# A four-layer graph network on one core: layer 3's normalised tile turned by VectorE and DMA, and the order searched anew

## The chip, the cores and the metric

The kernel runs on one core of a Trainium2 chip. The metric is the device time of one execution in microseconds; the time before is 3502.5 us, the median of three runs (3499.14 to 3503.25). A profile of one more execution of the same program shows what each engine did.

## The reference

The input is `x`, 64 graphs of 256 nodes with 256 features in float32, and `adj`, 64 adjacency matrices of 256 x 256 int32. Four layers follow each other. Each normalises x over its features, applies relu, computes an update from the result h and the adjacency, and adds it to x.

```python
h = jnp.maximum(_layernorm(x, axis=-1), 0.0)
x = x + _L0_gnn_ref(h, adj, ...)   # 8-head masked softmax attention, output projection
...
x = x + _L1_gnn_ref(h, adj, ...)   # one-head additive attention, softmax over the rows, elu
...
x = x + _L2_gnn_ref(h, adj, ...)   # 3 steps of: messages A^T h W, then a GRU cell
...
x = x + _L3_gnn_ref(h, adj, ...)   # 4-head additive attention
```

Layer 3, which the change is about, is this:

```python
f = (jnp.einsum('bni,oi->bno', node_feats, W) + b).reshape(B, N, H, c)
s_src = jnp.einsum('bnhc,hc->bnh', f, a_src)
s_dst = jnp.einsum('bnhc,hc->bnh', f, a_dst)
logits = jax.nn.leaky_relu(s_src[:, :, None, :] + s_dst[:, None, :, :], ALPHA)
logits = jnp.where(adj_matrix[..., None] == 1, logits, NEG_INF)
probs = jax.nn.softmax(logits, axis=2)
out = jnp.einsum('bijh,bjhc->bihc', probs, f)
```

## The kernel before

The graphs are worked on in 32 pairs. A pair's x is one tile of 128 partitions x 1024 values: four groups of 128 nodes (two for each graph), 256 features each. Six such tiles exist, so up to six pairs are under way at a time. Other buffers come from pools as well: 21 tiles `w4` of 128 x 1024, 8 PSUM banks, 8 DRAM tiles `turn` for turning a tile through DRAM, and more (SLOTS, line 324).

**Turning a tile.** Products on TensorE need operands with features on the partitions, while normalising and softmax need nodes there. A tile can be turned in two ways. On TensorE, `nc.tensor.transpose` turns a 128x128 block into a PSUM bank, from which ScalarE or VectorE copies it out (line 664 for a normalised tile, with relu in the copy at 676 or 677). Or VectorE transposes 32x32 blocks (line 734, 755 or 768) and `through_dram` (line 720) writes the tile to DRAM in one transfer (line 723) and reads it back in four (line 726), which puts the blocks into place. `by_dma` (line 580) decides for each layer and pair: before, layers 0 and 2 take the way through DRAM for the normalised tile, and so do the GRU step's results ("2m"), in each case for all pairs but the last.

**The stages of a pair.** `norm_relu` (line 584) computes statistics on VectorE (592, 594), the reciprocal root on GpSimd (605, 606), and the scaled tile on ScalarE (619) or VectorE (625). It also issues the load of the adjacency (704). Layer 0 forms queries, keys and values (823, 699), the scores (844, tiles of 32 rows), the masked row minimum on VectorE (792), the exponentials on ScalarE (799), the division (876), turns the result through DRAM, and multiplies with the values in tiles of 32 columns (896); 911 is the output projection. Layer 1 has its products at 1017 and 1031. Layer 2 runs three steps: messages (1101), gates with the weights `whhT` and `giT` (1124), and the update (1149 to 1192); its result is added to x at 1221. Layer 3 (line 1225) multiplies the turned tile with W (1246), spreads one score to all partitions through DRAM (928, 936), forms logits and softmax (1277, 792, 799), turns the exponentials through DRAM, and forms the context in tiles of 64 columns (1300). Its result is turned back: a block transpose (1316), a 256 KB write (1320) and four reads (1323). Then `to_x` (1334) multiplies each head by the reciprocal of its softmax sum and adds it to x, in 8 instructions of 128x64 for each graph. The last pair's layer 3 uses TensorE for all its turns.

**The order of the work.** All of this is recorded first as a list of tasks (`plan.add`), each with the engine that may run it, a duration in microseconds, the buffers it uses and, for a transfer, a latency. The order of all tasks over all engines is not written out in the program: it is the result of a search, stored as a compressed string ORDER, with the choice of engine for each task that has several. `Plan.order` unpacks the string, sorts the tasks, goes through them with the durations, and gives each buffer the slot that comes free first. Every engine then issues its instructions in that order; all transfers go through the SP queue. The planner's view of a transfer is in this line, with SLOW = 1.4:

```python
t.end, t.engine = begin + us + t.latency * self.SLOW, engine
```

Of the kernel before, what the change touches and what calls it, by code (L numbers as in the profile page):

```python
# [13 lines left out]
FR = mybir.dt.float32r  # L14
# [23 lines left out]
class Task:  # L38
    __slots__ = ("pair", "forms", "form", "bufs", "rank", "stage", "mode", "before", "end", "engine", "latency")


class Plan:
# [3 lines left out]
    SLOW, SWITCH = 1.4, 0.19  # L46

    ORDER = (
        "c-rlI2Y_T%m3Ezb?|b*<S2=f8=iJki6U>kqh9FVNf`bxFxW-*vcSZDHRM1_+qO7>AxQa?rRz*hQNQMbaf?;y%?&;}R)m{1B{}wPamAa>TNTS"
        "m)-PKk1y?fvJ&iT%F&b^JSGxS-RKJ<7U64EsK?}%Y0r__{_Uj7&8U+e;ezYbn~=5t^|8eRr>NB1*mH>9AK9{<I<U8uk53z1K3{?Urxi6f5Qp"  # L50
        "L85YtP5wZZ@SSCI;`VY0Agr<EfaDCgryJGK(Ao(E2C;o?=fQTkzr5V#aIKFa#Nd>s5>pHWbHM_>$|64w^(2_*j$qy`J@LNQq%PQK<`58FlP~"
        "$<JEDo{#ESp7_z7CW5ce#tL#Wpf@eThz7NR=y5@}0kspJe)|$O2>umFYylNhQC@e^E0f2Te%2str2(qFGNjvbbF{ERFq&#gcA0UPGtUekhbK"
        "zCz59hn_{m1x->~fk2lAxkK5COxG4=@6cgSv;5{*V21VINSEKmd^d+9c365cS8qMSiO%HR#X)9F3MmcZz7~N&rF#&^iobfD~eh`*egbjDW`9"
        "1wS{JiI^V?IT=JRjmdV)g^7hzpaA%lfSSNr6;c5exo0VTkD-*FLK(XqA;2x$VwXE4A>5x~^YO*0(Ns-Z8EHf?cZ}|Ro=W?iIjO%@f|j(N{lF"
        "^(Ajq;fOlUfYEj(+LOfBDnTFVj;Q&WGwgD4zb1BRd<TA*t~%`kGt2w)}I5IoJfU%t^TWxRn?#&#&*@MA(e$GCUezY|mvYHL7g>}m7T`VRq?#"
        "a<*~S1$!06|SaI?rJwi9ylkKX#1j1Nx0A@quIKznsS=L2V;Z&PAbFBXrLcJR&!}8hnz5uH%%izMqC^snY$s33X}lK3a9*;8%pV-Ifm4%U)_x"
        "!v(Fa)2us26bgfXND^Q&Nztg2Q0e*rn0&ExS>iPJmXFqv@0JYL4h{#cZeLy;qL^qH+&|oLB3o4(bHBDH6%#>CNU<?50oe=H?IHP%m{&@H_nZ"
        "U!II>@i49iv=xMzdVQQZPr%aX5Pe47jt9<K967n%TJDNE!Q04f)RNPi=lS*54@PpFx3^R4Cro4H!p<EG+`(kG?#Y#x`{+E@56gMjq1B2~Um>"
        "bqF<vnA2P!fE}x;HW0G22i)-3=_a^+bB?is>pKB%xbhS3JwgIokd=nuCI}6&&Ax2&dP5A1tLC}#hTzXcZCs_7tZCo=q^JUd=C(oC*T6n%8ke"
        "l>02SQmwaBj8y?YmI-Oo-${sA|cZ=hX2c7ss^i;+lfk^n^dkter)^oGs=fUqDf<R~)X?u#Y<38>t42()L!R9}>PAmd&|I8F%S5_f)-5l?-Dh"  # L60
        "zNyzG?6ue0|v;yvR{sGjh+DCUMk!Vu48L<gtn@n+2LLn%tQQ^-F`@1V4n%!mTJ&GEW6w)9)wf84MWY}hpwOlKU&`+=Hsd!$aq9~?Z*EmxNbW"
        "}4d8}Lc|f{Gr(f(`bdn@K8TNoL!f_gv$7g0_)-?i@A(G?PgII8f7!&FR<g#Zn2q`h7=op{d_{({ZZ%ub)(S|M+XrrXs*PX2+9Evlc1!_qgt1"
        "N4^fN*JYqxHw^+)ZQF>`gNP!a^=|`JZ(Jp`?-XA*O{X6Ysf{hbzpiM=U3@lODV5W2FAmzpmdASmznV=R^DE+SjmuuP@c4r)22Zeeu5Ub@~~?"
        "?XF?#y4iM4Blxnrq?Kv|GjWuXTq78Zmjg1#<4AR+hE#BgxJxi!c^SkERc5(gN+v+gh{B?{!5+mTr`nlW&UUy3?)->Zt14E*2sas;m&@c{nGF"
        "OIA_N3M=XUHRVaW4dbf*-h*xMkE+XF)5tU4i}eGDFeD?NS}UA;6ie#sLj-;SckImx#jALdsG!5O1z9yhu^EZ8Bgc)0mtx@5dG?~&On35~Yk?"
        "F!gM9<z(aSaPM`VK=2S>;4@+<k2B8WcR3$)L*hIH6ZQ<hbVYKoW(5Gy3c3vEP*g;+SJn8W8Vv=nD;WMBR)=q(rCi2DG=^R2tOZ`u`d=U5e%K"
        "_nCY6W0BIaaqb~4dlR*}F%^L;U6q}a)y=IN@pi3we8Z0LG>?T01z{DVb=4*B~j9&c!20@v9u>~*AW6BewH@h|1cg}N;J@f9C{!AFkQgxiD*$"
        "^PR{VU%;^LM{i!4CSluby__bCSfAK=2afJ8N-=;DgpgYhb?P!|-k0%3ShCn6qoY7u*g^kBPLqujZsW4Njo_^!j$Bbi!%7S>jhZY6DmRbnq-~"
        "8T193rCIK@nMo)Rs<m>kW;PXIh(EpLnpcC!zt^2;7X|ysyls-;6rqmN;Zt`lLa$yhyY6!GlVfZ2u;Jb2cYai<7jBZzGeEi@iRTfpli52xo+p"
        "&{<^jcNALBWy4%O_G!Q<XC>)EK_sz>()XwU^B@<(>bj`qDy?qQ1_gz15(DN+ow5ex5daGpS0y<i{+qiMOUP@`I+W1JIRy|Le;$3qtBaSR4H5"  # L70
        "%`l4Z73(Z`rLLAo$P(4?lwK`=;QymOM632FArVCoiCDNauCgucT&#$Oc(7WOpFyTHLhB+t_wJ~Mx>benLqMGTNjfhALPho{a)*qFN;XT^JY2"
        "6G)_8S|M(aLT<gE{(KDZG=w10WX~tUS5HmIXCa&3iDqMTN$8&4gx6enX^)_w0&t=5AP~)`q{u|VjWq@P$Ipqd|^?<<XkT&JU2fE-C9((J)Is"
        "AcUfO-ha%f`MK@c?|G@r==~$37|%oxtM8z%xJew!o~FZk`3zXm1D`F7T$6)m;LRv;>^1DVGJq;PnFO2}Sq04DPsw2->2ayUu-L*>d!0_&$6_"
        "KQlUa%MuWzo~4(cDMl2$&W~XM5?~IkA6gfldEz<&RFO)i7=g{r;PCf_*MZ%s;WhGff$&UQM`66F$qGG)&VomvGw4C}gbM|n)z%9TBJgZ&hzk"
        "?Dy*`OEjXn!wjVHc(f#HUv+=C<`?hr9}Swz$lNfRec19{UOj++A`qBF?>7xDZ-(bL9_4FO7%HK=p%%pod?BW@5H<8|=AZQ~S4!_*|uW@U}Jd"
        "l7~1G|EL#LTR<UDR-Q5N`g}?;JoLvesYcTl?8EbXn>VVVumyz%1B_rT~0^btDL;=WB>bK4qx1^EnD`$$+hNUJGf{6=ubn_p>3XN`Xt%>#_=~"
        "ogO1&ajE?0&o|Hs6{NE3D-uY`UH&X4Vnjd#v6Lt)@`>wg?L_CvpTE=lT$Bnx^;)9@Ag2iPA8t{W8hvgJ`_E?a(eDm`JZRh63+`lmQtrMOR^@"
        "JB@NIUHx+VYfd`KQ;ymy|iahgJF5Q`Ver@~4L11Py3GyLnCyK$|j68PjrbZ2MD9E=YhM1s$MZUEsm6O|@$vY*8EYet_%5Om?oYmrrvh{U7@h"
        "Wa^a5K)>A6^o*f}05-_bpnwkD3F4^Z+H~3`36M~?ql1``6b#r!IF2qWLib~hrV|aIv<y*rk~<p8<`it`UX*Zbx|)mD5KdWL(2-Mi1S~UY1ff"
        "M6VXN>^otOp7!8Ik2+*h99YBHS6Xda}a?=lZt@(2ZD_jmNj4p&x)|M{Axe#0LgG6ZRtWEu&3`_}wrLLNBv>%aK<@-OFQyz`Em(sRB8$OX0Xb"  # L80
        "@O&!Ot~T5|Mb!)@BK#WqYyE&-7iK#^QMLcZOo0nbl>^#DV3(@cs}w6?X$<}M$8KxYLfhCTcEE?s#~%m^V!g6?1~B|A~H#GNa`F&X3x#wD^2P"
        "E>017*`b$a&f5bFxe+AhSP8!{L#ohmsyAykS+dS98ciYb9(Rz*?)i_&`pPdE@5_fX-(F{~vl3L?-pFJXbLW0tVgg`A%b|A<gkpb+-3VL3F#a"
        "yXCV_L~6up62T>EiDxXL*q-D-yU#PJc}yDu&%Sn3v_GBc{n7k<r?I?g%D|cSVK(k(ixp3e3fUgDE6q5y3%t5N4!}){dZL2?-~HIx7U3d0bjH"
        "i76I^W{~<C2BiH>3ho?qXI8F{XofUMgNp8jl(zB=lV`M;f=nqx&&N(h5JcSpFwMPN2r%ixFJNVTU;`KN{l|`?1Y)yRaV?6lKsh>aT+6IqJ_#"
        "O%(SxzMXKV&JX_)8CdU);QrXDw;Id|a;D=zvRp3dD2h$hqyr;s!2Mvb1n@Ew%6Q1F=eDT#lqb7rU~p!$;EQd?hb^LFlR%bZpJQ+d>sM2VMHy"
        "gUF;3ri`FawSd21njU>iM#!_0QYWTT#F8ZD2k{y*#}E}PtVys{Ts7?3QwU1v=~15=n|7719!B#3>O+k5ah{?G@=vT4>?cpG2}vVZg;ndN4)N"
        "&D_OIiKrO&u8uh4(5%MII6#o?~_-x-T-t&l^>lr_hw9&vCMevHAN8G%kk`**Pi?xP~!AlC6uc%>2Z`k7=P-E`6EFjsB%^VPH5mj=)Y3t?8qg"
        "Ko%#k7p>hp2`9&s_%;HSu_Ag2qwBa@co^e9oE9baEw&#cJ7*)rwKn(nm&);qtDIi(jsV2q?tBR!}xUj0AhafX=w;gYM?7O)(I}O}hX16`GLd"
        "`a}drpUSC08gKsO!uh7iFw9vB|MQqs!`;xUWwL$w7$e8Ow(L{g>M!gaLU@1Np+mE^&!A}y2d+!}{tujkkZ|RS<DcAPkX#6K+`4Y9%;h+l&xV"
        "aNr~d$gF*gE7!eC64ozaXXuQ-;IdXjPp)R0d|J0+ejxb`{!ehG=l=Z*z-o|9RA`uf&w@J09`T#svRMtf_tI{uiSJ;|V9=ohgR;WA{7BfHn-o"  # L90
        "bDrta$Yf@2G{gc+Qd0<A2&0G7fhJN!PNqm6Vmp?9iM1yhDYI2MHb|g8;`XPcwX`wZa~l5L%IY8Ze$K6Xklf>dhCcdio1dyo+dCQ7B`0O$@-O"
        ")n2}OS0Bdz=L;r1h%qfl9ld>Y#&sgo+a221bCIvziHSmm<Fb8$FM4H|Gp%?L}WvKgne1+}tG|jbvB5Q&UKCYC1DtevZkxU*cjp`_BB52u_$N"
        "L6bb_9ULBe{$2rCFTe=@PUgw-Jzs9@z2ih8oO}BL1oGGb^!~k>v=QvFtcX7=;DH%hb<D??ugAjc1smYJs&bJxgK5Eu&YSraA=-S8jC$ZZnOf"
        "9O+0A^$rEeGVTK1J-_t<i0fijGUNU+q9e62?i}uIN0i2}4mqyFDXin{XQG(Vv_(==Zio)~)S$kec<}>pzx^xt21AF>4O|R4o$24ItJfo_N8y"
        "E{+N6Y!PduA2PQLDUAiMTa9HMSQh~gqW(|*y0d?fn&05ou3Q^Ij)s_yC^n*DGM`nh<r<aa6iokE1f#hnxa1YQW>ur6|Z5@Vi@adS-Lv?n^S7"
        "3kOlDIP;S#UT~>J)npQM7YuvrtP0O@<U9~7_J+s#Sn4F$kl7PJP0yIo1xic1NAW>$BW2rD(+vsrjbbUei9a7b^_8DY~<A3FskZKl=7ZMIUNn"
        "v`S#bU3-^Y0*MR?jlh^YSJ*_^^1)3cMU5(A$!gHsm59h0cZ~f-lrV}`70BbJlJnvjk5{l!?J^%XD>G^mvevCGMI=J*Ep))X?M4E}?4jFSL1t"
        "-3C$s>;<E=<+)o;o4*fZNLxWz!XX{_}xY5$Ix<J#_Z9*K%G}k_sRX_X0bOaOQkw9)I=}7ipZnhzhTGWv(X>Yuus8Y2E1s)Vq-F1vqXMd<DJ>"
        "p8#j$rG0a03op;_x|;h0Z0GbFKyI;JlT+D?W0FoqG3f&bgte`HKQBHyUlf2Rt91?<<cSt_W)p(<U#@K*l4iT_(Jukjrz8N=h7@ems25;)JMh"
        "X|rwd1sP^;!hXqZ!&%eSlE90d;y@$Ys}OtB@COWAWm%2Z&%C{rGkPzK4IzZ9j$-;c9ralIGDYP=Bzq;$?L^asFn%-q*ZK6loDhD0mJac<rZg"  # L100
        "X5=Q1)9Z_<U%=dA8t;~S?hA~s=vvZ<>C-sd-}H^4ukf+vxeLH%yGorG1b9Mmq!Wk&u*yMyNl-@f<jB5*8X7U<vLuq=ghC|;hBR+;Afw_>$r|"
        "PoqmCR@P6zUxcBn>;4~uWq!;fo0h^u+Rxt9aiJ0Mz`m!}&cX<b0;&hUVUEBF>Lyvp&F{|gP$>Wg4@zry9))*HBf;>Ebq8*&D2=|8tFX|XcK2"
        "yx;Z9{u#z;WBz*Te0nHbJw0QEFP30+N37G{xIMHY;w2hii$8H^Qh8nb9~VhG91cM6a=@z!1W{jt9C?jpBI*LzloMbu=Z}6=9rv;l<|daGn#n"
# [88 lines left out]
    def pair(self):  # L192
        self.pairs.append([])

    def add(self, forms, reads=(), writes=(), latency=0.0, claims=(), mode="full"):

        t = Task()
        t.pair, t.forms = len(self.pairs) - 1, [forms] if isinstance(forms, tuple) else forms
# [84 lines left out]
def tile_adj_preln_d4(  # L283
# [103 lines left out]
    def w4():  # L387
        return buf("w4")
# [1028 lines left out]
```

## Time and profile before

| what | value |
|---|---|
| median of three runs | 3502.5 us |
| the profiled execution's own time | 3501.53 us |
| its span, first to last instruction | 3499.7 us |
| mean granted TensorE clock | 0.993 |
| ScalarE busy | 2522.0 us |
| GpSimd busy | 453.1 us |
| transfers: moved, share of the 16 DMA engines' span | 749.98 MB, 69.3% |
| writes `turn` of 512 KB, reads of 128 KB | 535, 2140 |

An engine's instructions run in the order in which they were issued, so one that waits holds up all behind it. In the timeline a line gives the start, the length, the engine, the program line, the operation and the tiles that it writes and reads; "x8" means that so many instructions were merged, and a bracket names the idle time before and what ended it. In a group's row the first number after the bar is the time in which at least one of the group ran, the second the mean of one in ns. A float32 matmul stands as two instructions in the profile, a transpose as one.

### The profile page before, as it was taken

What the parts mean: (1) busy time and instruction counts of PE and PEld (TensorE: products, weight loads), DVE (VectorE), ACT (ScalarE), POOL (GpSimd) and SP (SyncE); (2) the same over time, 40 slices, a digit from 0 to 9 for tenths busy, and PEclk for the clock granted to TensorE, in tenths of its full rate; (3) what the DMA queues carried; (4) which work ended last, traced back from release to release, by engine and by line L of the source; (5) the groups of instructions that cost most, each with busy time, mean ns of one, the idle gap of its engine ahead of it and who ended that gap; (6) DMA issues with size and microseconds to landing.
All of it is one profiled execution on the core that took longest, in us unless ns stands there. A gap on an engine that the chain in (4) does not pass through costs nothing.

```text
span 3499.7 us, 53732 instructions
## 1 busy us (share of the span) xinstructions
PE 3433.5 (98%) x14784; PEld 1931.6 (55%) x14784; DVE 3078.1 (88%) x9047; ACT 2522.0 (72%) x6739; POOL 453.1 (13%) x497
## 2 busy tenths in 40 slices
PE   8899999999999999999999999999999999999997
PEld 5555555555555555555555555555555555555554
DVE  8788998999999989999899888999889989889767
ACT  7756786766776777777767777778777768668545
POOL 1010110111111111111111111111011111011010
PEclk9999999999999999999999999999999999999998
DMA  8655877777677777777776777777677776576444
GB/s 287 209 150 167 248 240 217 224 229 228 212 217 233 226 222 235 223 225 225 218 230 215 228 227 216 235 230 234 214 228 216 234 224 218 183 220 201 155 131 136
DMA packets 596081, 753.41 MB, mean 215 GB/s; under 512 B 99012, under 2 KB 507076, under 8 KB 595780
## 3 DMA queue, kind: packets, MB, share of 16 engines
q1 hardware_dynamic: 595780, 749.98, 69.3%
q8 instruction: 118, 1.93, 0.2%
q14 instruction: 183, 1.50, 0.1%
HBM read 426.78 MB, written 314.59 MB: 212 GB/s over the span
## 4 chain that ended last, share of the span: by engine, by line
PE 64%; DVE 7%; DMA 3%; ACT 2%; issue 1%; SPq 1%; POOL 0%; DVEq 0%; ACTq 0%; POOLq 0%
PE ps L1124 37%; PE ps L823 4%; PE ps L1101 4%; PE ps L1246 3%; PE ps L844 3%; PE ps L1300 2%; PE ps L699 2%; PE ps L1031 2%; PE ps L896 2%; PE ps L1017 2%; PE ps L911 2%; DMA w<-turn 2%; DVE w L792 1%; DVE w L954 1%; DVE x L1334 1%
## 5 line engine op out<-in xcount | busy, mean ns | idle before, releaser
L1124 PE MATMUL ps<-w,whhT 128*128 128x512 f32 x2304 | 1071.2, 594 | 1.2 <-DVE mx L792 1.0
L1124 PE MATMUL ps<-w,giT 128*128 128x512 f32 x2304 | 1064.9, 593 | 0.0
L799 ACT ACTIVATE w<-w,mx 128x256 f32<-128x256 f32 x1536 | 759.2, 499 | 45.2 <-DVE mx L792 43.7
L1124 PEld LDWEIGHTS ps<-w,giT 128*128 128x128 f32 x2304 | 435.9, 190 | 534.5 <-issue 511.2
L1124 PEld LDWEIGHTS ps<-w,whhT 128*128 128x128 f32 x2304 | 430.4, 190 | 496.3 <-issue 451.4
L734 DVE STREAM_TRANSPOSE w<-w 128x1024 f32<-128x1024 f32 x380 | 466.4, 1234 | 45.2 <-ACT w L876 25.7
L417 ACT COPY w<-ps 128x512 f32<-128x512 f32 x431 | 244.2, 579 | 198.1 <-PE ps L1300 79.0
L792 DVE CUSTOM_DVE_ANT_0 w<-ps,mask 128x256 f32<-128x256 f32 x1024 | 370.8, 417 | 14.7 <-PE ps L844 12.6
L876 ACT ACTIVATE w<-w,rz 128x256 f32<-128x256 f32 x678 | 292.4, 498 | 88.4 <-DVE rz L869 85.1
L619 ACT ACTIVATE w<-x,rs 128x256 f32<-128x256 f32 x464 | 244.7, 591 | 93.3 <-DVE rs L611 88.9
L799 ACT ACTIVATION_READ_ACCUMULATOR w<-w,mx 128x1 f32 x1536 | 293.4, 191 | 0.0
L1181 POOL TENSOR_TENSOR w<-w,w 128x512 f32<-128x512 f32 x86 | 114.0, 1332 | 1147.9 <-PE ps L1124 368.4
L1277 ACT ACTIVATE w<-w,f 128x256 f32<-128x256 f32 x512 | 219.5, 499 | 16.1 <-DMA w<-row 10.0
L1101 PE MATMUL ps<-part,part 128*128 128x256 f32 x1536 | 228.8, 299 | 1.8 <-DVE part L1091 1.7
L605 POOL TENSOR_SCALAR rs<-mv 128x4 f32<-128x4 f32 x129 | 40.9, 317 | 1368.0 <-DVE mv L594 1301.1
L1149 ACT ACTIVATE w<-ps,brz 128x512 f32<-128x512 f32 x192 | 129.3, 677 | 123.1 <-PE ps L1124 113.4
L1101 PEld LDWEIGHTS ps<-part,part 128*128 128x128 f32 x1536 | 197.3, 190 | 32.1 <-issue 18.3
L792 DVE CUSTOM_DVE_ANT_0 w<-w,mask 128x256 f32<-128x256 f32 x512 | 196.4, 428 | 13.3 <-ACT w L1277 12.4
L1176 ACT ACTIVATE w<-w,bih_sb 128x512 f32<-128x512 f32 x192 | 136.5, 716 | 97.4 <-DVE w L1172 97.3
L592 DVE BATCH_NORM_STATS2 st<-x 128x6 f32<-128x256 f32 x512 | 189.1, 411 | 10.8 <-DMA x<-in_x_dram 8.2
L1163 ACT ACTIVATE w<-ps,brz 128x512 f32<-128x512 f32 x192 | 129.2, 677 | 75.5 <-PE ps L1124 73.1
L1154 DVE SCALAR_TENSOR_TENSOR w<-w,w 128x512 f32<-128x512 f32 x192 | 132.6, 692 | 44.4 <-ACT w L1149 28.1
(117 smaller groups left out, 5132.7 us busy)
## 6 DMA issues: line engine op xcount, KB each, us to landing
turn<-w SPq DMA_DIRECT2D x535, 512.0 KB
w<-turn SPq DMA_DIRECT2D x2140, 128.0 KB
w<-in_adj_dram SPq DMA_DIRECT2D x128, 512.0 KB
w<-row SPq DMA_DIRECT2D x64, 512.0 KB
x<-in_x_dram SPq DMA_DIRECT2D x64, 256.0 KB
out_dram<-x SPq DMA_DIRECT2D x64, 256.0 KB
turn<-w SPq DMA_DIRECT2D x62, 256.0 KB
w<-turn SPq DMA_DIRECT2D x248, 64.0 KB
```

The costliest lines, as they stand in the source:

```text
L417: (A, act(n), lambda: nc.scalar.copy(dst(), src())),
L592: nc.vector.bn_stats(st()[:, t, :], tok(xt())[:, t, :])
L619: nc.scalar.activation(tok(xn())[:, t, :], tok(xt())[:, t, :], func, bias=rs()[:, 1, t : t + 1], scale=rs()[:, 0, t : t + 1])
L734: add((V, dve(T * N), lambda: nc.vector.transpose(blocks(), blocks())), writes=[e])
L792: nc.vector.tensor_tensor_reduce(row, src, mask, scale, 3.0e38, ALU.add, ALU.min, mn)
L799: nc.scalar.activation(row(e, r), row(e, r), AF.Exp, bias=mn()[:, r : r + 1], scale=-1.0, accum_out=zs()[:, z0(r) : z0(r) + 1])
L823: mm(ps(), w[:, k, o * P : (o + 1) * P], wide(hT, k), start=k == 0, stop=k == 1)
L876: op(row, row, rz()[:, r : r + 1])
L1101: mm(ps()[:, o * N : (o + 1) * N], chunk_of(part(), h.mixed, c, o), tok(ams[g](), N)[:, c, :], start=i == 0 and c == 0, stop=i == 1 and c ...
L1124: mm(ps(), w[:, k, c0 : c0 + P], wide(src, k), start=n == 0, stop=n == 2 * len(terms) - 1)
L1176: (A, act(N2, 1), lambda o=o, hn=hn: nc.scalar.activation(at_o(hn, o), at_o(hn, o), AF.Tanh, bias=bih_sb[:, 4 + o : 5 + o])),
L1277: nc.scalar.activation(dst, src, AF.Prelu, bias=f()[:, t, D + h : D + h + 1], alpha=ALPHA)
```

## The change

The change has four parts.

1. Layer 3 joins the layers whose normalised tile is turned through DRAM, for pairs 0 to 30. For them the eight transposes of TensorE and the two evictions go; a block transpose of 128x1024 on VectorE (line 768 before), one write of 512 KB, four reads of 128 KB and two relus from SBUF (648, 649) come.
2. Layer 3's context is formed in tiles of 32 columns in place of 64: twice as many matmuls with half the columns each.
3. The end of layer 3 is written in another way: the block transpose puts the blocks down in another arrangement, two multiplications of 128x256 with the reciprocal sums replace the factor in the 8 small instructions, and one addition of 128x512 on VectorE or GpSimd updates x.
4. The planner has other durations, and transfers share a queue in it: each occupies the queue for its own time and lands 3.2 us after that. The whole order was searched anew with it, and with it the choice of engine for every task that has several. In the new order VectorE scales 126 groups of 256 features (48 before), ScalarE 386 (464).

The branches for `early` in layer 0 are never taken, since EARLY is 0.

```diff
-    SLOW, SWITCH = 1.4, 0.19
+    SWITCH, LANDING = 0.19, 3.2
...
-            t.end, t.engine = begin + us + t.latency * self.SLOW, engine
+            if engine == "SP":
+                free["DMA"] = max(free["SP"], free.get("DMA", 0.0)) + t.dma
+                t.end, t.engine = free["DMA"] + self.LANDING, engine
+            else:
+                t.end, t.engine = begin + us, engine
...
-    TURNED = ("0", "2", "2m",)
+    EARLY, LATE = 0, 1
+    TURNED = ("0", "2", "3", "2m")
 
     def by_dma(l, p):
 
-        return l in TURNED and p < B // 2 - 1
+        if l == "2m":
+            return p < B // 2 - 1
+        return l in TURNED and EARLY <= p < B // 2 - LATE
...
         d = buf("turn")
-        add((SP, 0.6, lambda: nc.sync.dma_start(d(), e())), reads=[e], writes=[d], latency=4.6)
+        add((SP, 0.41, lambda: nc.sync.dma_start(d(), e())), reads=[e], writes=[d], dma=1.32)
...
-                reads=[d], writes=[(eT, b)], latency=3.8,
+                reads=[d], writes=[(eT, b)], dma=0.47,
...
-                            mm(
-                                pso()[j * C3 : (j + 1) * C3, k * N : (k + 1) * N],
-                                f()[:, 2 * g + c, h * C3 : (h + 1) * C3],
...
+                            for r in range(0, C3, 32):
+                                mm(
+                                    pso()[j * C3 + r : j * C3 + r + 32, k * N : (k + 1) * N],
+                                    f()[:, 2 * g + c, h * C3 + r : h * C3 + r + 32],
...
-            add((PE, 1.75, product), reads=[*eT, (f, 2 * g), (f, 2 * g + 1)], writes=[pso], claims=[oT], mode="halves")
+            add((PE, 1.75, product), reads=[*eT, (f, 2 * g), (f, 2 * g + 1)], writes=[pso], claims=[oT], mode="columns")
...
-                        e2().rearrange("p (b x i) -> p b x i", b=4, i=32), oT().rearrange("p (x b j) -> p b x j", b=4, j=32))),
+                        e2().rearrange("p (b c k i) -> p b k c i", b=4, c=2, k=2), oT().rearrange("p (k c b j) -> p b k c j", k=2, c=2, b=4))),
...
-                for c in range(2):
-
-                    def to_x(c=c, g=g, o=o, rz=rz):
-                        for h in range(H3):
-                            ap = o().rearrange("p (j a x i) -> p j x a i", j=2, a=2, i=32)[:, h % 2, 2 * (h // 2) + c]
-                            xh = tok(xt())[:, 2 * g + c, h * C3 : (h + 1) * C3].rearrange("p (a i) -> p a i", a=2)
-                            nc.vector.scalar_tensor_tensor(
-                                xh, ap, rz()[:, H3 * c + h : H3 * c + h + 1], xh, ALU.mult, ALU.add
-                            )
-
-                    add((V, H3 * 0.14, to_x, True), reads=[o, rz], writes=[(xt, g)])
+                def divided(o=o, rz=rz):
+                    for j in range(2):
+                        oj = o().rearrange("p (j a y i) -> p j a y i", j=2, a=2, i=32)[:, j]
+                        rj = rz().rearrange("p (y j) -> p j y", j=2)[:, j]
+                        nc.vector.tensor_tensor(oj, oj, rj.unsqueeze(1).unsqueeze(3).to_broadcast([P, 2, 4, 32]), ALU.mult)
+
+                add((V, 0.7, divided, True), reads=[rz], writes=[o])
+
+                def to_x(eng, g=g, o=o):
+                    xa = xt()[:, g * N2 : (g + 1) * N2].rearrange("p (y a i) -> p y a i", y=4, a=4)
+                    eng.tensor_add(xa, xa, o().rearrange("p (a y i) -> p y a i", a=4, y=4))
+
+                add(either(0.0, to_x), reads=[o], writes=[(xt, g)])
```

## The prediction

> **What bounds the kernel now.** I read the page first: busy time, then the waits. TensorE is busy for 3433.5 us of a 3499.7 us span and idle for 66.2; no other engine has so little room.
>
> ```profile
> span 3499.7 us, 53732 instructions
> ...
> PE 3433.5 (98%) x14784; PEld 1931.6 (55%) x14784; DVE 3078.1 (88%) x9047; ACT 2522.0 (72%) x6739; POOL 453.1 (13%) x497
> ```
>
> Next, the busy time by stretch (columns: stretch, length, busy us of each engine with instructions, granted clock, DMA share, GB/s).
>
> ```profile
> 0.00:400.00 400.00, 373.41 (x1765) 220.36 (x1766) 335.73 (x1057) 279.04 (x775) 48.70 (x61) 0.98 0.67 208
> 400.00:3200.00 2800.00, 2781.38 (x11988) 1560.07 (x11987) 2524.01 (x7424) 2081.84 (x5562) 379.44 (x407) 1.00 0.72 222
> 3200.00:3500.00 300.00, 278.75 (x1033) 151.12 (x1031) 218.38 (x568) 161.14 (x404) 24.91 (x30) 0.96 0.51 158
> ```
>
> TensorE's idle time is 26.6 us in the ramp, 18.6 in the long middle, 21.3 in the last 300 us. In the middle it is idle for 0.7% only: there, work taken off TensorE shortens the kernel directly, as long as nothing new makes it wait. The transfers' share of 0.72 and VectorE's 2524 of 2800 are the next resources. The third view is TensorE's timeline in the middle, where the same pattern returns every 104.9 us (2020.54 to 2125.49 for the removed transposes).
>
> ```profile
> 2125.49 1.04 PE L664 MATMUL ps<-ident,w 128*128 128x128 f32 x8
> 2126.36 1.88 PE L1124 MATMUL ps<-w,whhT 128*128 128x512 f32 x4
> 2128.08 1.88 PE L1124 MATMUL ps<-w,giT 128*128 128x512 f32 x4
> 2129.80 3.62 PE L1017 MATMUL ps<-w,w 128*128 128x256 f32 x16
> 2133.25 3.72 PE L1246 MATMUL ps<-w3a,w 128*128 128x264 f32 x16
> ```
>
> The eight transposes (L664) hold TensorE from 2125.49 to the next start at 2126.36: 0.87 us. The product that needs them (L1246) starts at 2133.25.
>
> **The change part by part.**
>
> *Transposes off TensorE.* Line 664 runs 272 times; 24 belong to the last pair and stay, so 248 go (31 pairs of 8). Start to start one costs 0.87/8 = 0.109 us: 248 x 0.109 = -27.0 us. The group's own row gives an upper bound, since its ends overlap the next instruction: 39.1/272 = 0.144, or -35.7. I take 27.0, because the start-to-start interval is what the next matmul gains.
>
> *Context in 32-column tiles.* 64 products with 16 narrow matmuls each in place of 8 wide ones. Layer 0's context already has that shape.
>
> ```profile
> L896 PE MATMUL ps<-w,w 128*32 128x256 f32 x2048 | 127.0, 391 | 15.3 <-DMA w<-turn 12.8 <-DVE mx L792 2.4
> ...
> L1300 PE MATMUL ps<-w,f 128*64 128x256 f32 x1024 | 119.0, 383 | 3.9 <-DMA w<-turn 2.0 <-DVE w L418 1.8
> ```
>
> Over the run the narrow form costs 127.0 - 119.0 = +8.0 us more for 64 products, but its row holds the ramp at clock 0.98. In the chain of waits, two narrow products take 3.59 us (at 2047.49) and two wide ones 3.60 (at 2087.74). I take 0; +8.0 is the other end.
>
> *Tile modes.* Counting in the built programs' issue order, TensorE changes between whole, row, column and half tiles 326 times before and 343 times after. Four gate matmuls ahead of a change last 1.81 us (2068.06 to 2069.87) where four others last 1.71 (2077.92 to 2079.63): 0.09 to 0.10 a change, 17 x 0.09 = +1.5 us.
>
> *Waits that go.* In the middle TensorE waits 2.3 us at L664 and 2.2 + 0.9 us at L1246 for its evictions. These 5.4 us go; the relu behind the new transfer is late next. I count half, -2.7, and keep 0 and -5.4.
>
> *VectorE.* Out: 496 small updates of x (L1334), 111.9 us. In: 124 multiplies on half tiles; the trace has none, the nearest rows are the add at L1221 (0.37) and half of L1352's 0.685 (0.34), so +46 (42 to 51); 41 of the 62 adds, which are L1045's shape at 0.69, +28 (the other 21 on POOL at 1.3); 31 block transposes at L768's 1.24, +38; 78 more scalings of x at L625's 0.41, +32; 61 more casts at 0.41, +25; relu from SBUF in place of PSUM, -5; other forms that the order picks (evictions, divisions, adds), together +9. Sum +61 us, that is 3139 us, while ScalarE loses about 107 (78 scalings at 0.53, 61 casts at 0.60, the rest small). All of it lies beside TensorE's work: per period VectorE has now 104.9 x 276/2800 = 10.3 us free and keeps over 7. Cost 0; without that cover it would be 2 us a pair.
>
> *Transfers and SP.* 31 more writes of 512 KB and 124 more reads of 128 KB: 32.5 MB on 750, +4.3%, so the middle's share goes from 0.72 to some 0.75. SP issues 155 more at 0.34 and 0.43 us, 64 us in all, or 2 a pair; it is a queue in order, and each new write waits at its head for VectorE's transpose. Behind it stand reads of layer 0's turned tiles, for which L896 waits, and adjacency loads. SP's waits for the like transpose of layer 2 (L768) were 206.7 us in 39 cases without TensorE paying for them, so I count 0.
>
> *The added path.* ScalarE finishes the normalised tile at 2123.68 and L1246 starts at 2133.25: 9.6 us, most of it the evictions' place in VectorE's queue.
>
> ```profile
> 2121.60 2.08 ACT L619 ACTIVATE w<-x,rs 128x256 f32<-128x256 f32 x4 [0.37 <-DVE rs L611]
> ```
>
> ```profile
> 2129.92 0.65 DVE L677 TENSOR_SCALAR w<-ps 128x512 f32<-128x512 f32 x1
> ...
> 2131.69 0.68 DVE L677 TENSOR_SCALAR w<-ps 128x512 f32<-128x512 f32 x1
> ```
>
> After: transpose 1.24, a write, a read, two relus of about 0.5. The longest-lived transfers of the chain bound write and read from above.
>
> ```profile
> 2987.02 6.27 DMA w<-turn
> ```
>
> ```profile
> 3185.46 6.47 DMA turn<-w
> ```
>
> That makes 1.24 + 6.47 + 6.27 + 1.0 = 15 us, 5.4 more than now. In issue order, TensorE's work between a pair's layer-1 product and its L1246, priced by start-to-start rows, is 321 us both before and after (mean of pairs 6 to 26), so the order gives this path no more room ahead of L1246; it shortens what follows instead (65.8 to 62.9 us from there to the context). The 5.4 us must come from slack ahead, such as the 6.7 us from the end of POOL's half of the update of x (2110.21) to the statistics (2116.88). I take it as covered; that is the weakest step.
>
> Two statements of the Trainium skill bear here, and no term uses them. After the row above (0.109 us a transpose): "VectorE: DVE Perf Modes", "Rules for kernel authors", speaks against the change: it sends a 128x128 transpose to TensorE where PSUM will do. Its table of three transpose paths has 390 ns (bf16) for one on TensorE; as an estimate from that figure 248 would free 97 us and the sum would be near 3404, but in this trace they overlap their neighbours. After the rows on transfers: "DMA: Bandwidth & Descriptors", "Anatomy of one DMA", fits 2.0 us plus bytes over 436 GB/s for the GpSimd-issued path; as an estimate a write would take 3.2 and a read 2.3, and the new path would fit into today's 9.6 us; under this kernel's load the chain shows twice that.
>
> *Start and end.* Both orders start with the same weight transposes and layer-0 work and end with the same unchanged last pair on TensorE: 0.
>
> **Sum.** -27.0 + 0 + 1.5 - 2.7 = -28.2 against the profiled execution's own 3501.5 us: 3473.3. That execution lies 1.0 us below the median 3502.5, which changes nothing here. I predict 3473; own range 3460 (-35.7 and -5.4, mode changes free: -41) to 3484 (context +8.0, no waits saved: -17.5). About 0.2%, 7 us, is what a measurement of this kernel can tell from no change.
>
> **Rivals.**
>
> *More is won: 3457.* The new order prices a shared transfer queue, and TensorE's longest waits are for turned tiles (L896: 12.8 us in 4 waits, 8.4 the longest, in the ramp). Apart from the first load (6.9) and the last 50 us (21.0), 38 us are idle; half gone is -19 in place of -2.7: 3457. Against it: the ramp's issue order is nearly the same.
>
> *Nothing is won: 3500.* The turned tile lands late by as much as the transposes cost, 25.5/31 = 0.82 us a pair on average. For it: the path is 5.4 us longer with no more room in the order. It is also what remains if VectorE, now 90% busy in the middle, delivers evictions later.
>
> *Slower: 3525.* One mechanism, at one place: the layer-3 product (L1246 now) waits in TensorE's queue for the turned tile, with the gates of other pairs behind it. Price: the mean wait of L896 for such a tile, 12.8/4 = 3.2 us. It decides from a mean of 0.82 us; in every second pair it gives 15.5 x 3.2 = 50, 3501.5 - 25.5 + 50 = 3526, in every pair 3575. Against it: in the middle, L896 waits for turned tiles only 3 times (4.3 us) although it needs 8 of them a pair.
>
> **How the numbers follow.** Forecast 0.55, more won 0.17, nothing won 0.12, slower 0.16. The first two are faster by over 0.2%: 0.72; same 0.12; slower 0.16. The range leaves out the slower case and the far edge of "more won": 3452 to 3504, taking in "nothing won".
>
> **What would show it.** Right: TensorE busy near 3408 us, 24 transposes left on the normalising line, the 104.9 us pattern down to about 104.0, the context row near 119 to 127 us. Wrong: a wait of the layer-3 product for the relu or its transfer in more than a few pairs; idle time of TensorE in the middle well over 18.6 us; VectorE over 93% there; narrow contexts at more than 1.9 us each.

## The result, and the profile after

The changed kernel takes 3511.6 us (median of seven runs, 3508.2 to 3521.1) against 3502.2 for the kernel before on the same chip: ratio 1.0032, 95% interval 1.0019 to 1.0044. It is slower by 0.3%; the prediction was 3473, with a range of 3452 to 3504. Program lines are 47 to 67 higher now: the message product 1101 is 1164, layer 0's context 896 is 958, the layer-3 product 1246 is 1309, the cast of a message part 1085/1086 is 1148/1149, the layer-3 logits 1277 are 1340.

The page of the changed kernel, span and busy time:

```profile
span 3513.7 us, 55132 instructions
...
PE 3419.8 (97%) x15560; PEld 1904.3 (54%) x15560; DVE 3139.7 (89%) x8937; ACT 2427.8 (69%) x6536; POOL 481.7 (14%) x520
```

The stretches (columns as before the change: stretch, length, busy us of TensorE, its weight loads, VectorE, ScalarE, GpSimd, then granted clock, transfer share, GB/s):

```profile
0.00:400.00 400.00, 381.38 (x1831) 222.96 (x1832) 351.52 (x1101) 284.17 (x791) 56.38 (x70) 1.00 0.71 223
400.00:3200.00 2800.00, 2752.08 (x12526) 1528.15 (x12525) 2554.29 (x7266) 1977.09 (x5330) 393.50 (x418) 1.00 0.76 230
3200.00:3515.00 315.00, 286.30 (x1205) 153.22 (x1203) 233.92 (x574) 166.53 (x416) 31.79 (x33) 0.95 0.53 170
```

TensorE's busy time fell by 13.7 us, about half of what was removed from it (3408 was forecast). A part of the other half is the way in which busy time is counted: the last matmul ahead of a wait counts to its end, though within a stretch the next would have started before that, and TensorE's work now stands in 106 separate stretches in place of 72 (counted in the traces). TensorE's idle time rose from 66.2 to 93.9 us, and nearly all of the rise is in the middle: 47.9 us in place of 18.6. VectorE's 3139.7 us and the transfers' share of 0.76 are what was forecast. So the work is as reckoned, and TensorE waits more. For whom? TensorE's waits from 400 to 3200 us (in total, times, longest):

```profile
PE ps L958 <- DMA w<-turn: 10.7, 7, 3.5
PE ps L1164 <- DVE part L1149: 4.4, 4, 2.4
PE ps L885 <- ACT w L700: 3.4, 3, 1.6
PE ps L1309 <- DVE w L701: 3.1, 4, 1.0
PE ps L1187 <- DVE w L1255: 3.0, 2, 1.9
```

No line carries it: many places wait a little, the layer-3 product (1309) in four cases only. TensorE's own view names VectorE and ScalarE; what *they* waited for is one view further. First ScalarE, before the change, its largest waits for transfers in the same stretch:

```profile
ACT w L648 <- DMA w<-turn: 4.2, 2, 2.6
...
ACT part L1085 <- DMA w<-turn: 3.7, 3, 1.8
...
ACT w L1277 <- DMA w<-row: 3.5, 3, 1.2
```

and after:

```profile
ACT w L1340 <- DMA w<-row: 51.8, 30, 5.9
...
ACT w L700 <- DMA w<-turn: 31.0, 19, 5.3
...
ACT part L1148 <- DMA w<-turn: 10.2, 11, 2.1
```

ScalarE reaches the logits of layer 3 (1340) before the spread row has landed 30 times in place of 3. Added up over the three compute engines, waits ended by a transfer in the middle grew from 31.2 us (32 times) to 130.9 (89 times). How such a wait holds up the next engine is seen in one stretch of the timeline:

```profile
861.22 0.38 SPq L999 DMA_DIRECT2D w<-row  x1
```

```profile
869.12 1.71 ACT L1340 ACTIVATE w<-w,f 128x256 f32<-128x256 f32 x4 [5.94 <-DMA w<-row]
870.46 0.43 DVE L844 CUSTOM_DVE_ANT_0 w<-w,mask 128x256 f32<-128x256 f32 x1 [3.50 <-ACT w L1340]
...
870.53 2.04 PE L958 MATMUL ps<-w,w 128*32 128x256 f32 x21 [3.52 <-DMA w<-turn]
```

The spread row is issued at 861.22 and ScalarE's logits start when it is there, at 869.12. ScalarE has then stood for 5.94 us with everything queued behind it, and VectorE's masked minima (844) for 3.50 us behind ScalarE. TensorE stands for 3.52 us at the same time, but behind a late turned tile of its own: how much of its wait came by way of ScalarE this stretch doesn't say.

The rows of the narrow contexts (out<-in, shapes, count, then busy us and mean ns of one):

```profile
L958 PE MATMUL ps<-w,w 128*32 128x256 f32 x2048 | 131.8, 388 | 15.8 <-DMA w<-turn 13.7 <-DVE w L820 1.2 <-ACT w L464 0.8
L1364 PE MATMUL ps<-w,f 128*32 128x256 f32 x2048 | 123.4, 387 | 10.6 <-DMA w<-turn 7.9 <-DVE w L465 1.9 <-ACT w L464 0.7
```

Layer 3's went from 119.0 to 123.4 us; but layer 0's (958), which the change doesn't touch, went from 127.0 to 131.8 as well. One matmul takes no longer in either order (388 ns in layer 0 after, 391 before). Layer 0's stand in 56 separate stretches in place of 43, layer 3's in 50 in place of 37 (counted in the traces), and each stretch ends with a matmul that runs out alone.

### The profile page after: what moved, and what is told of

Its sections match the earlier page's. It is cut to its first block, busy times and chain, and to the rows that moved or that the text cites. A ratio compares the mean times of both kernels' runs of the same rounds, so it can differ in the third digit from the quotient of the medians.

```text
span 3513.7 us, 55132 instructions
## 1 busy us (share of the span) xinstructions
PE 3419.8 (97%) x15560; PEld 1904.3 (54%) x15560; DVE 3139.7 (89%) x8937; ACT 2427.8 (69%) x6536; POOL 481.7 (14%) x520
## 5 line engine op out<-in xcount | busy, mean ns | idle before, releaser
L464 ACT COPY w<-ps 128x512 f32<-128x512 f32 x453 | 254.7, 580 | 239.7 <-PE ps L1164 81.0
L844 DVE CUSTOM_DVE_ANT_0 w<-ps,mask 128x256 f32<-128x256 f32 x1024 | 372.5, 415 | 13.3 <-PE ps L906 12.7
L938 ACT ACTIVATE w<-w,rz 128x256 f32<-128x256 f32 x634 | 276.6, 498 | 112.7 <-DVE rz L932 109.3
L1244 POOL TENSOR_TENSOR w<-w,w 128x512 f32<-128x512 f32 x102 | 133.7, 1314 | 1229.4 <-ACT w L1239 858.3
L671 ACT ACTIVATE w<-x,rs 128x256 f32<-128x256 f32 x386 | 205.1, 591 | 98.0 <-DVE rs L663 96.5
L1164 PE MATMUL ps<-part,part 128*128 128x256 f32 x1536 | 247.2, 309 | 11.6 <-DVE part L1149 4.4
L1250 DVE SCALAR_TENSOR_TENSOR w<-w,w 128x512 f32<-128x512 f32 x192 | 142.3, 744 | 20.1 <-ACT w L1226 9.5
```

What stands on the lines that cost most here:

```text
L464: (A, act(n), lambda: nc.scalar.copy(dst(), src())),
L671: nc.scalar.activation(tok(xn())[:, t, :], tok(xt())[:, t, :], func, bias=rs()[:, 1, t : t + 1], scale=rs()[:, 0, t : t + 1])
L844: nc.vector.tensor_tensor_reduce(row, src, mask, scale, 3.0e38, ALU.add, ALU.min, mn)
L938: op(row(e, r), row(e, r), rz()[:, r : r + 1])
L1164: mm(ps()[:, o * N : (o + 1) * N], chunk_of(part(), h.mixed, c, o), tok(ams[g](), N)[:, c, :], start=i == 0 and c == 0, stop=i == 1 and c ...
L1250: (V, dve(N2), lambda o=o, z=zt[o], u=u: nc.vector.scalar_tensor_tensor(wide(u, o), z(), 1.0, wide(u, o), ALU.add, ALU.mult), True),
```

## Theories

- **Thin margin.** The new order was searched with other prices (`LANDING = 3.2` behind a queue, in place of each latency times 1.4). It puts users so close behind what they use that a late transfer, or an engine a little behind, stalls a queue. The edits are sound; the order is the loss.
- **Load.** Layer 3's 4% more transfers make every transfer late.
- **VectorE.** 61 us more on VectorE make it deliver late.

All runs in one table. "Idle" is TensorE's; waits for transfers are those of TensorE, VectorE and ScalarE together from 400 to 3200 us. Ratios are to the kernel before, run beside.

| run | us | ratio, 95% interval | TensorE busy, idle | idle 400-3200 | waits for transfers |
|---|---|---|---|---|---|
| before | 3502.2 | 1 | 3433.5, 66.2 | 18.6 | 31.2 |
| after | 3511.6 | 1.0032 (1.0019-1.0044) | 3419.8, 93.9 | 47.9 | 130.9 |
| b_load | 3530.6 | 1.0093 (1.0079-1.0107) | 3443.3, 90.5 | 33.6 | 75.9 |
| b_load2 | 3536.1 | 1.0103 (1.0089-1.0117) | 3441.9, 94.7 | 41.4 | 86.2 |
| b_tox32 | 3490.7 | 0.9974 (0.9965-0.9984) | 3431.9, 59.7 | 13.9 | 32.6 |
| b_half | 3497.0 | 0.9992 (0.9983-1.0001) | 3430.9, 65.2 | 18.4 | 22.6 |
| a_half | 3487.8 | 0.9973 (0.9959-0.9986) | 3408.5, 77.4 | 33.5 | 58.2 |
| a_l3pe | 3538.3 | 1.0108 (1.0092-1.0123) | 3448.5, 89.7 | 41.8 | 101.9 |
| a_tight | 3519.9 | 1.0049 (1.0036-1.0063) | 3417.4, 98.2 | 49.9 | 133.2 |
| a_vec | 3493.2 | 0.9977 (0.9965-0.9989) | 3416.7, 77.0 | 34.7 | 145.2 |
| a_land | 3481.3 | 0.9943 (0.9931-0.9955) | 3402.2, 77.2 | 30.1 | 57.8 |
| a_order | 3461.8 | 0.9892 (0.9878-0.9905) | 3397.0, 61.2 | 13.3 | 69.1 |
| pe_robust | 3477.6 | 0.9935 (0.9922-0.9947) | 3424.3, 47.8 | 8.5 | 57.8 |
| a_robust | 3453.1 | 0.9856 (0.9841-0.9870) | 3398.5, 54.8 | 16.3 | 50.4 |

## Experiments

### The two small edits without the new order: b_tox32

The order and engine choices of the kernel before; only the context in 32-column tiles and the new end of layer 3:

```diff
-                            mm(pso()[j * C3 : (j + 1) * C3, ...], f()[:, 2 * g + c, h * C3 : (h + 1) * C3], ...)
+                            for r in range(0, C3, 32):
+                                mm(pso()[j * C3 + r : j * C3 + r + 32, ...], ...)
...
-                    add((V, H3 * 0.14, to_x, True), reads=[o, rz], writes=[(xt, g)])
+                add((V, 0.7, divided, True), reads=[rz], writes=[o])
+                add((V, 0.7, lambda to_x=to_x: to_x(nc.vector), True), reads=[o], writes=[(xt, g)])
```

> The order of the kernel before, engine for engine, with two of the three edits: the context of layer 3 in 32-column tiles, and the update of x as two multiplies and one add on VectorE in place of eight small updates (a saving of some 112 - 46 - 43 = 23 us of VectorE). Layer 3's tile stays on TensorE. All theories of the loss expect no loss here: 3495 to 3508. If the narrow context costs what the rows of the whole run say (+8.0 us) and the mode changes 1.5, it is 3512 at most; if these two edits are the loss, it is 3520 or more (9.1 us loss of the change plus the 28 us forecast would be 3540).

3490.7 us, 9 us faster than before and better than any theory had it. The context's row of this run:

```profile
L1301 PE MATMUL ps<-w,f 128*32 128x256 f32 x2048 | 119.4, 384 | 2.7 <-DVE w L418 1.6 <-DMA w<-turn 1.2
```

119.4 us against 119.0 for half as many wide matmuls: narrow tiles cost nothing, as forecast. With it VectorE has 14.6 us less to do (3063.5 against 3078.1), and TensorE's idle time falls by 6.5 us, 4.7 of them in the middle. The likeliest reason is VectorE's lighter load, which the prediction counted at nothing; no run takes it apart from the other differences of the new end.

### The added transfers alone: b_load and b_load2

To the kernel before, at the place of layer 3's turn, one write and four reads for which nobody waits:

```diff
+                if base == "3" and p < B // 2 - 1 and i == 0:
+                    nc.sync.dma_start(dst_d, giT.rearrange("p l f c -> p (l f c)")[:, 0 : T * N])
+                    reads((0, 1))
...
+                if t == 0 and not last:
+                    reads((2, 3))
```

> The order and the work of the kernel before, and beside them layer 3's new transfers alone, with nobody waiting for them: per pair (0 to 30) one more write of 512 KB at the place of the removed turn, and four reads (two there, two at the layer-3 product) of 128 partitions x 864 bytes, 108 KB each in place of 128 KB. Theory 'thin margin' (the new order puts the users of transfers so close behind their issues that late ones stall the queues; the added transfers themselves matter little): 3500 to 3508, TensorE's idle time from 400 to 3200 us at most 24 us (before 18.6). Rival 'load' (4% more transfers make every transfer later, and that is the whole loss): the idle time there rises by about 29 us, to 45 or more, and the time to 3525 to 3535. Rival 'VectorE' (61 us more on VectorE make it deliver late): 3500 to 3506, as the first.

> As b_load, but the extra reads take their bytes from the adjacency input and nothing is prepared for them, since in b_load's trace 6.7 us were lost in the first 135 us, where a memset and a write were added ahead of the first loads. 'Thin margin': the rest of b_load's loss lay before 1100 us and in the last 450, so the time is 3510 to 3525, and TensorE's idle time from 1000 to 3200 us stays at 16 or less (before 9.3, b_load 15.0). 'Load' as the cause of the changed kernel's loss in the middle (31.0 us idle there): 25 or more.

3530.6 and 3536.1 us: about 30 to 36 us slower, as much as "load" asked for, though not where it asked for it. Stretches of b_load2, whose start has no addition (before: 396.67 of 400 busy from 800 to 1200 and 1195.31 of 1200 from 1200 to 2400):

```profile
400.00:800.00 400.00, 385.25 (x1642) 215.05 (x1641) 354.96 (x1026) 291.97 (x780) 60.07 (x67) 0.99 0.79 234
800.00:1200.00 400.00, 387.85 (x1633) 214.66 (x1632) 352.94 (x1049) 278.32 (x752) 55.20 (x60) 0.98 0.78 224
1200.00:2400.00 1200.00, 1191.60 (x5180) 668.23 (x5179) 1081.80 (x3178) 894.90 (x2381) 166.75 (x173) 1.00 0.79 234
2400.00:2960.00 560.00, 560.00 (x2443) 313.59 (x2443) 506.87 (x1491) 429.14 (x1151) 68.41 (x72) 1.00 0.80 232
```

Where the old order runs in its steady pattern (1200 to 2960 us), the higher share of 0.79 costs 3.7 us in all. Most of the loss is made before: the ninth pair's first layer-3 product starts at 1207.8 us in place of 1179.2, and up to there TensorE waits 7.4 us for the relus behind turned tiles at layer 0's queries and keys (1.2 before). So more transfers do hurt where an order has no room for them; the margin theory's times were missed in both runs, and b_load's idle time in the middle, 33.6 us, lies between the bounds of the two theories (24 and 45). The experiment also adds 26 us of waits at the head of SyncE's queue (14 cases, at the extra reads), so the price is not that of the bytes alone. It doesn't explain the changed kernel, whose loss is made elsewhere: its layer-3 product of the fifth pair starts 15.7 us ahead of the kernel before (737.2 against 752.9), that of the 19th 15.0 us behind (2253.2 against 2238.2).

### Half the turned bytes: a_half and b_half

```diff
-        d = buf("turn")
-        add((SP, 0.41, lambda: nc.sync.dma_start(d(), e())), reads=[e], writes=[d], dma=1.32)
+        d, n = buf("turn"), 128 if len(plan.pairs) < 10 else 64
+        add((SP, 0.41, lambda: nc.sync.dma_start(d()[0:n, :], e()[0:n, :])), reads=[e], writes=[d], dma=1.32)
```

and the reads likewise.

> The changed kernel, whole order kept, but from the tenth pair on every turn through DRAM writes and reads back only half of its bytes (64 partitions of the write, 64 KB of each read), so half of each turned tile is stale and the output is not the reference's. All else is the same work. 'Thin margin' and 'load': TensorE's idle time from 1000 to 3200 us falls from 31.0 to 12 us or less, and the time by about 20 to 25 us, to 3487 to 3492. 'VectorE': idle time stays at 25 or more and the time at 3505 to 3512.

> The kernel before with the same halving of the turned bytes from the tenth pair on (output not the reference's). All theories: little to gain, since its idle time from 1000 to 3200 us is 9.3 us in all: idle there 6 to 9 us, time 3496 to 3502. If the gain is as large as that of the changed kernel under the same halving (20 us or more), the margin of the orders isn't what sets them apart.

By the ratios the changed kernel gains 21 us (1.0032 to 0.9973), the kernel before 3. So the changed order loses to late transfers what the old one doesn't. But a_half still idles for 22.3 us from 1000 to 3200 (31.0 without the halving), with transfers at 0.53 there: that lies between the bounds of the theories, and a part of the loss isn't the transfers.

### The new order without layer 3's turn: a_l3pe

```diff
-    TURNED = ("0", "2", "3", "2m")
+    TURNED = ("0", "2", "2m")
```

All other tasks keep their place in the order; TensorE's eight transposes and the evictions stand where the block transpose stood.

> The changed kernel's own order, all positions kept, but layer 3's tile turned on TensorE again: per pair 8 transposes and two evictions right behind the normalised tile, in place of the block transpose, the write, the four reads and the two relus from SBUF. 4% fewer transfers. 'Thin margin' (the order itself): TensorE's idle time from 400 to 3200 us stays at 40 or more, and with 27 us more work on TensorE the time is 3525 to 3545. 'Load': idle time falls to about 20 and the time is 3505 to 3515.

3538.3 us, 41.8 us idle in the middle. The transfers are those of the kernel before (0.73 of the middle) and the loss is nearly whole: 101.9 us of waits for transfers against 31.2 in the old order under the same load. The added transfers are not needed for the loss; the order makes it. Against b_tox32, which has the same edits and transfers, the new order with its engine choices costs 0.0134 (47 us). And with the order held, the turn through DRAM brings 0.0076 (27 us), though a_l3pe's order was searched for the other way of turning.

### Only the order: a_order, a_tight, a_land, a_vec

Four kernels with the changed kernel's tasks, its engine for each and its transfers, byte for byte; only ORDER is another. In each, single tasks were moved from the changed kernel's order on, and a move was kept if the planned spans (the plan's own sums, not times of the chip) didn't grow in sum. They differ in the prices of those plans:

- a_tight: landing 3.2 us, the changed kernel's own price.
- a_land: landing 3.4 and 4.4 us.
- a_vec: landing 3.2 us; VectorE and ScalarE at their plain prices and 5% up.
- a_order: landing 3.4 and 4.4 us, and 3.6 us with VectorE and ScalarE 4% up.

> The changed kernel with the same tasks, the same engine for each task and the same transfers; only the order is another: from the new order on, single tasks were moved within their engines' queues (TensorE's by 1.6 places on average, VectorE's by 5, SyncE's by 7), and a move was kept if the sum of three planned spans didn't grow: landings priced 3.4 and 4.4 us in place of 3.2, and 3.6 us with VectorE and ScalarE priced 4% up. 'Thin margin': TensorE's idle time from 400 to 3200 us falls from 47.9 us to 20 or less and the time by 30 to 45 us, to 3467 to 3482. 'Load' and 'VectorE' (same bytes, same work of each engine): idle time stays at 40 or more and the time above 3500.

> Order only, as a_order (same tasks, engines and transfers as the changed kernel), but searched with the changed kernel's own price for a landing alone, 3.2 us. TensorE's tasks move by 2.1 places on average, VectorE's by 7, SyncE's by 9: more than in a_order. 'Thin margin': no room is made, so the loss stays: 3495 to 3520, TensorE's idle time from 400 to 3200 us 35 us or more. Rival 'a_order's search was merely longer': 3457 to 3475, idle time there 20 or less.

> Order only, searched with landings priced 3.4 and 4.4 us and VectorE and ScalarE at their plain prices. If room for late transfers is what a_order gained by: 3460 to 3475, idle time from 400 to 3200 us 20 or less. If it was the room for a slower VectorE and ScalarE (its third price): 3490 or more.

> Order only, searched with the landing at 3.2 us and VectorE and ScalarE at their plain prices and 5% up: room for these two engines, none for late transfers. 'Thin margin' of transfers: 3490 to 3515, idle time from 400 to 3200 us 30 or more, with waits for transfers of turned tiles and of the rows that are spread ahead of them. 'VectorE': 3460 to 3475.

a_order takes 3461.8 us: 1.4% less than the changed kernel (0.9892 against 1.0032), with the same work, and better than the 3467 to 3482 that 'thin margin' expected. Transfers take 0.78 of the middle, more than the 0.76 of the changed kernel. Its middle, and its largest waits there:

```profile
400.00:3200.00 2800.00, 2786.67 (x12757) 1550.04 (x12756) 2607.05 (x7378) 2015.75 (x5427) 399.48 (x425) 1.00 0.78 235
```

```profile
PE ps L878 <- DVE w L694: 4.1, 5, 1.7
PE ps L1157 <- DVE part L1147: 1.0, 3, 0.4
PE ps L1180 <- DVE mx L837: 0.9, 2, 0.7
...
PE ps L951 <- DMA w<-turn: 0.4, 1, 0.4
```

Layer 0's context (951 here, 958 after) waits for turned tiles for 0.4 us in place of 10.7, the message product (1157) 1.0 in place of 4.4 for its worst line. VectorE is at 93% (2607 of 2800), which the prediction named as a sign of trouble, and nobody is worse off for it.

a_tight moves tasks further than a_order, at the old price, and is no better than the changed kernel (1.0049): the gain isn't that of a longer search. The other two take it apart. a_land, where landings alone get room:

```profile
400.00:3200.00 2800.00, 2769.89 (x12630) 1538.25 (x12629) 2582.22 (x7340) 2005.53 (x5413) 403.32 (x423) 1.00 0.77 233
```

```profile
ACT w L1333 <- DMA w<-row: 29.2, 22, 7.8
...
ACT w L693 <- DMA w<-turn: 6.1, 8, 1.8
```

a_vec, where VectorE and ScalarE alone get room:

```profile
400.00:3200.00 2800.00, 2765.33 (x12605) 1540.16 (x12603) 2564.13 (x7308) 1990.19 (x5361) 392.50 (x417) 1.00 0.76 232
```

```profile
ACT w L1332 <- DMA w<-row: 71.9, 28, 6.7
...
ACT w L692 <- DMA w<-turn: 9.8, 11, 2.0
```

Waits for transfers fall to 57.8 us in a_land and stay at 145.2 in a_vec, as each was meant to do. Against a_tight's 1.0049, room for landings brings 0.0106 (37 us), room for the two engines 0.0072 (25 us), both 0.0157 (55 us). Neither theory's numbers for a_land and a_vec hold alone: a_land lies above its 3460 to 3475, and a_vec within the 3490 to 3515 of thin transfers but well below a_tight. The margin was thin on two sides: against late transfers, and against VectorE and ScalarE taking a little longer than planned. How large each side is stays rough: every set of prices gave one order, and how far two searches at the same prices lie apart is known from one pair only (the changed kernel and a_tight, 0.0017). Nor does a run show what a second planned span brings by itself; a_tight was searched with one, a_land and a_vec with two, a_order with three.

### What the turn is worth with room: pe_robust

The diff of a_l3pe, with an order searched like a_order's. The engine choices changed with it: over 100 tasks of pe_robust run on another engine than in a_l3pe, 35 of them on GpSimd in place of VectorE.

> The changed kernel with layer 3's tile turned on TensorE again (as in the kernel before), the two other edits kept, and an order found in the same way and with the same prices as a_order's. It says what the turn through DRAM is worth when both orders leave room for late transfers. If the forecast's first term is right (248 transposes, 27 us), this run is 22 to 32 us above a_order, near 3500. If the transfers give the gain back even then (load), it is within 8 us of a_order. If it is faster than a_order, the turn itself is the loss.

```profile
PE 3424.3 (99%) x15808; PEld 1920.3 (55%) x15808; DVE 3094.3 (89%) x8869; ACT 2428.2 (70%) x6539; POOL 522.6 (15%) x555
```

```profile
PE 3397.0 (98%) x15560; PEld 1893.8 (55%) x15560; DVE 3140.6 (91%) x8937; ACT 2428.2 (70%) x6536; POOL 480.2 (14%) x520
```

The first line is pe_robust, the second a_order. The 248 transposes show as 27.3 us of TensorE's busy time, and as 28.7 us between a_l3pe and the changed kernel; the forecast's first term was 27.0. That the first is so near is luck: of the busy time 23.2 us in pe_robust and 10.3 in a_order lie in stretches of half clock (last section), which is 6.5 of the 27.3. a_order idles 13.4 us more (61.2 against 47.8), so the turn brings 15.8 us (0.0043), less than the 22 to 32 expected. Why is open: 8.6 of the 13.4 us lie before 400 and after 3200 us, and the engine choices differ too.

### The best order found: a_robust

ORDER and engine choices together, with landings at 3.4, 4.6 and 5.2 us and once 3.6 with VectorE and ScalarE 5% up.

> The changed kernel's tasks with order and engine choices searched together (788 tasks change their engine), with landings at 3.4, 4.6 and 5.2 us and once 3.6 us with VectorE and ScalarE 5% up. Meant as the best version: 3448 to 3462, TensorE's idle time over the run 45 to 60 us (a_order 61.2). If the room beyond 4.4 us is worth nothing, it equals a_order within 5 us.

3453.1 us, 1.4% below the kernel before and faster than all others. It is 9 us below a_order by the medians and 13 by the ratios, with ScalarE at 2482.7 us (2428.2 in a_order) and VectorE at 3096.8 (3140.6). How much of that is the wider room and how much the engine choice was not taken apart.

## Why the prediction was wrong

- **Transposes off TensorE, -27.0.** Right in size: 27.3 and 28.7 in the two pairs of kernels, 21 and 32 where the time at half clock is taken out.
- **Context in 32 columns, 0, and tile modes, +1.5.** The first is right (119.4 against 119.0 us). Of the second nothing is seen: b_tox32, whose context has the new tile mode, has 1.6 us less busy time on TensorE.
- **Waits that go, -2.7.** Wrong. The waits at the transposes went, those of the layer-3 product stayed (3.1 us for the relu in the middle), and others took their place.
- **VectorE, "Cost 0".** The size was right (3139 forecast, 3139.7 measured, and the terms hold one by one: the 124 multiplies take 48.5 us, the 31 block transposes 38), the price wrong. It was read from a share: 10.3 us free in a period "hide" 2 us. Free time in a period doesn't say that a result is there when it is wanted; the order decides that. a_vec against a_tight shows what the order's lack of room for these engines cost, some 25 us.
- **Transfers and SP, "so I count 0".** Share right (0.75 forecast, 0.76), price wrong in the same way. The zero rested on how the *old* order bears its transfers. In the new order transfers are awaited 89 times in place of 32 in the middle, and a_land against a_tight puts 37 us on the lack of room for them. The *added* transfers are not what costs it: without them (a_l3pe) the loss stays.
- **The added path, "I take it as covered; that is the weakest step".** It held: the layer-3 product waits for its relu in 4 cases of the middle, and a_l3pe, without that path, loses as much.
- **The sum** is the step that failed. It treated the order as neutral, as a list of edits, and has no term for it; the two zeros above follow from that. Measured, the new order with its engine choices costs 47 us with the tile still turned on TensorE (b_tox32 to a_l3pe). The prices that changed with it stood in the diff and entered no term: a read of a turned tile was planned to land 3.8 x 1.4 = 5.3 us after its issue, now 0.47 + 3.2 = 3.7 us with an empty queue, while the trace of before had a read of 6.27 us in its chain (and one of 6.47 at 3070.38, which the prediction passed over). A search that is told 3.7 can fill the gap with other work; a_tight, searched at that price, has the loss, and a_land, at higher ones, has less of it.
- **The rivals.** "Slower" had the sign, at the wrong place: not one product but many queues. Its price of 3.2 us for one wait was too high as a mean: layer 0's context waits for a turned tile 7 times in the middle, 1.5 us on average and 3.5 at the longest. "Nothing is won" named late VectorE deliveries, which were the smaller part of the cause.
- **The signs.** Of the signs of being wrong, "idle time of TensorE in the middle well over 18.6" is the one that came true clearly (47.9). "Narrow contexts at more than 1.9 us each" did by a hair (123.4/64 = 1.93), but not for the narrow form (119.4/64 = 1.87 in b_tox32): it is the layer's more numerous separate stretches. From the 9th to the 25th pair the layer-3 products follow each other in 106.4 us on average (starts at 1177.7 and 2880.7), 105.4 before (1179.2 and 2866.3) and 105.0 in a_order (1153.3 and 2833.2).

Put together from the ratios: the small edits -0.0026, an order with room in place of the old one, with other engine choices (b_tox32 to pe_robust), -0.0039, the turn -0.0043, and the order that came with the change, against a_order, +0.0140. By the other path, with the order that came: the small edits -0.0026, that order +0.0134, the turn -0.0076. Either way the edits alone bring 24 to 36 us, and the order costs 35 us against the old one by the first path, 47 by the second, and 49 against a_order, which has the same engine choices. That the 24 lies near the forecast's 28 is luck: 9 of it come from the small edits, which were counted at +1.5, and the turn brings 15, where 27.0 and 2.7 were expected.

Left open: which of the late transfers are late by the engines that carry them and which by SyncE's queue; no run separates the two.

## What to carry to other kernels

When a fixed order over in-order queues is searched anew, its prices are part of the change: compare each new price with the latest case in the trace, not with the mean, and search with room for transfers and for engines that run a few per cent late. Here kernels that differ in no instruction, only in order, lie 55 us apart (ratios 0.9892 and 1.0049). When TensorE's waits are spread thin over many lines, look one engine upstream: here it was ScalarE's waits for transfers that had grown, from 22 to 103 us.

## What the runs showed of the hardware

A gap in TensorE's work can cost more than itself. Stretches of 2 us of the changed kernel around one of the waits of the middle (columns as above; the granted clock is the third value from the right):

```profile
2170.00:2172.00 2.00, 1.09 (x6) 0.61 (x4) 2.00 (x12) 0.60 (x2) 0.00 (x0) 1.00 0.49 143
2172.00:2174.00 2.00, 0.47 (x2) 0.30 (x2) 1.97 (x7) 0.99 (x4) 0.00 (x0) 1.00 0.63 185
2174.00:2176.00 2.00, 1.90 (x18) 1.68 (x22) 1.97 (x4) 2.00 (x10) 0.00 (x0) 0.82 0.04 8
2176.00:2178.00 2.00, 2.00 (x13) 1.35 (x10) 2.00 (x9) 1.54 (x5) 0.00 (x0) 0.50 0.46 190
2178.00:2180.00 2.00, 2.00 (x9) 1.25 (x7) 2.00 (x8) 1.12 (x4) 0.00 (x0) 0.82 0.21 77
```

TensorE waits 2.37 us here, and a little later its clock is halved for about 3.4 us (0.18 x 2 + 0.5 x 2 + 0.18 x 2 = 1.7 us of work lost). In the middle this happens five times in the changed kernel, twice before, never in a_order. In the changed kernel it follows single gaps of 1.92 to 3.52 us four times, and once it begins among three shorter ones that add up to 2.0 us; but one gap of 2.25 us (1925.0 to 1927.3) is followed by none, so the length of a gap alone doesn't decide it.

Over the whole run, the last 300 us included, 33.3 us of the changed kernel's busy time lie in such stretches, 34.6 before and 10.3 in a_order. So the clock is no part of the difference between before and after, but it is a part of why 15560 matmuls keep TensorE busy for 3419.8 us after the change and for 3397.0 in a_order: of the 55.5 us between the two spans 32.7 are idle time and 22.8 busy time, and half of 33.3 - 10.3, some 11.5 us, is the clock. The rest is not measured by itself; TensorE's work stands in 106 separate stretches against 71, and at the end of each the last matmul runs out with nothing behind it. An estimate from the rows: gates of four matmuls last 1.88 us and follow each other every 1.72, and a narrow matmul lasts 0.39 where 2048 take 123.4, so a run-out is 0.16 to 0.33 us, and 35 more are 6 to 11 us.

The clock is not the extra in the two context rows of the result: a_order has no such stretch in the middle, and its rows are 128.4 and 122.5 us.

The Trainium skill, "TensorE: Matmul & The Clock Gate", "HAM oscillation — how this bites in real kernels", has the clock fall after gaps in TensorE's work above about 3.4 us; here it fell after one of 2.37 us.
